# Layer 2's ends: adjacency pieces of the next diffusions loaded further ahead, into the memory of the keys

## The chip, the cores and the metric

The kernel runs on one core of a Trainium2 chip. The metric is the device time of one execution in microseconds (us). A core has TensorE (PE in the profile; its weight loads are PEld), VectorE (DVE), ScalarE (ACT), GpSimd (POOL) and SyncE (SP); SP does no arithmetic here and issues most of the DMAs. Each engine takes its instructions in order.

## The reference

N = 4096 nodes, D = 256 features, an adjacency of zeros and ones. Four layers, each closed by x = layernorm(x + f(x)). Layer 0 is graph attention with 8 heads, layer 1 a product with the adjacency, layer 3 a mean over neighbours with weights. The change lies in layer 2, which is cut here to what matters:

```python
R = S + eye(N); R = R / R.sum(-1, keepdims=True)     # S is the adjacency
Z = 0; Xf = X; Xa = X
for n in range(2):
    A = top_p_attention(Xa, W1, W2, W3)   # softmax of q k^T, only the largest probabilities whose sum
                                          # reaches 0.9 are kept, and renormalised
    Xf = R @ Xf                           # "diffusion"
    Xa = A @ Xa                           # "attention"
    Z = Z + Xf @ U1[n].T + Xa @ U2[n].T
h = X + Z                                 # then a layernorm of h
```

Layer 3 then needs adj @ x for the new x.

## The kernel before, in words

**Tiling.** The 4096 rows are 32 blocks (NB) of 128. In layer 2 the method `layer2` runs two steps, and in each a loop over the blocks b (b = 0 to 30 in the loop, block 31 after it). For a block, 4096 scores lie in one of three buffers `es`; `scores` (L1070) makes those of block b + 2 with matmuls of the queries `q` with the keys `kT`, a tile of 128 x 4096 numbers of 4 bytes (2 MB). `nucleus` (VectorE) finds the cut of a row and clears what lies below; `turn` (L1402, L1404) transposes four 128 x 128 parts of `es` on TensorE and copies them by ScalarE, and `gather` (L1411) multiplies them with X into the PSUM bank `ps_a`. That takes eight sub-steps s = 0 to 7 for a block.

**Pieces.** Beside it runs a diffusion: block b + 2 in step 0, b + 3 in step 1, with `XD` (32 chunks of 128 x 512, the features in two parts) as the moving operand. The adjacency lies in DRAM (`adjs`, with the identity added). A *piece* is four chunks of it, 128 x 512 numbers, 256 KB. `adj_product` (L170 to L180) loads a piece on SP (L177) into the ring `adj_piece` of three buffers, and TensorE multiplies it with four chunks of XD (L180). SP issues its DMAs in order: where a piece has no free buffer, SP waits, and what follows on its queue waits too.

**The ends.** When the last diffusion of a step is through, the first diffusions of what comes next are begun: in step 0 blocks 0 to 2 of step 1, in step 1 blocks 0 to 4 of layer 3. The list `todo` (L1688 on) holds the pairs (block k, piece g) in their order: 21 in step 0, 35 in step 1. `early` (L1619) goes through it. It loads two pieces ahead (`piece`, L1600, into the same ring), and each `next(beside)` in the loop (L1742) issues one more load and multiplies one piece (`times`, L1609). How many pieces fall into which sub-step is written out by hand in `pieces`. In step 1 adjacency pieces on the diagonal need the identity taken off again; GpSimd does that (L1602), and `piece` issues it right after the load. XD is refilled for the new product with `reload` (L1263, on SP), in the order of the table `freed`, which gives for a block and a sub-step the rows to load.

**The flag and the general way.** `settled` (L1291) tests whether the fast way of finding the cuts was right for all rows. Its last parts are two transposes on TensorE (L1314, L1319), a reduction, and a DMA of a row of flags to DRAM (L1323). Then every engine loads the flag (`flag = nc.values_load`, L1809) and branches in `mend` (L1265, L1269): only when the flag is 0 are blocks done again in an exact way, which needs `kT`. In the executions shown the flag isn't 0. `mend` of step 1 also uses `kT` as space for pieces.

**After the branch.** In step 0, `reload` fetches the last four rows of XD, and three pieces (k, 7) finish the diffusions of blocks 0 to 2 (loop over k, L1813 on); then come the last block's attention and the keys of step 1 (`keys`, L941, which writes `kT` anew). In step 1, `early` goes on with pieces 26 to 34 beside the last block's attention; ScalarE unpacks the adjacency of block 5 of layer 3 into `kT` (`cast3`, L1880), and layer 3 (L1956) follows.

**What sets the order.** Inside `tc.manual_schedule` (the loop over b; in step 1 the part after the branch too) the instructions of the five engines stay in the order of the code. Outside it a planner orders them by estimated costs and times; it may also put an instruction from behind the branch ahead of it, if nothing in the branch touches its data. An instruction that depends on what the branch reads or writes stays behind it.

Of the kernel before, what the change touches and what calls it, by code (L numbers as in the profile page):

```python
# [9 lines left out]
F32 = mybir.dt.float32  # L10
# [13 lines left out]
P = 128  # L24
# [31 lines left out]
class Net:  # L56
# [809 lines left out]
    def layer2(self):  # L866
        nc, tc, NB, D, X, N = self.nc, self.tc, self.NB, self.D, self.X, self.N
        A = 64
        HALF = N // 2
        with ExitStack() as ctx:  # L870
# [6 lines left out]
            dram = ctx.enter_context(tc.tile_pool(name="l2d", bufs=1, space=DRAM))  # L877
# [18 lines left out]
            kT = rows2.tile([P, N], F32R, name="kT")  # L896
# [30 lines left out]
            xfd = dram.tile([NB, P, 2, D], F32, name="xfd")  # L927
            xtd = dram.tile([NB, P, 2, D], F32, name="xtd")

            rowd = dram.tile([1, NB + 1], I32, name="rowd")  # L930
            XD = self.XD
            def at(b):
                return bass.ds(b, 1)
# [325 lines left out]
            def reload(src, a, b):  # L1259

                for k in range(a, b, 4):
                    to = min(k + 4, b)
                    nc.sync.dma_start(XD[:, k:to].bitcast(F32), src[k:to].rearrange("b p s d -> p b s d"))  # L1263

            def mend(step, row, flag, e, r, made=()):  # L1265


                spare = es[(NB - 2) % 3][:, :N]
                with tc.If(flag == 0):  # L1269
                    with tc.For_i(0, NB - 1, 1) as b:  # L1270
                        with tc.If(nc.values_load(row[:, at(b)], min_val=0, max_val=1) == 0):
                            e2, Z = exact_scores(b, spare)
                            r2 = exact_nucleus(e2, Z)
                            if step == 1:
                                finish(b, whole(closing(b, attention(e2), r2, bases(b))))
                            else:
                                store(b, attention(e2), r2)
                    with tc.If(nc.values_load(row[:, NB - 1:NB], min_val=0, max_val=1) == 0):
                        e2, Z = exact_scores(NB - 1, e)
                        nc.vector.tensor_copy(r, exact_nucleus(e2, Z))  # L1280
                    if step == 1:
                        reload(xtd, 0, NB - 4)
                        for ps, b, g, first in made:
                            if first:
                                nc.tensor.matmul(ps, kT[:, :P], XD[:, 0].rearrange("p s d -> p (s d)"),
                                                 start=False, stop=True)
                        for i, (ps, b, g, first) in enumerate(made):
                            a = kT[:, i % 8 * 512:i % 8 * 512 + 512].rearrange("p (k i) -> p k i", k=4)
                            times(ps, piece(step, b, g, a), g, first)
# [36 lines left out]
            def exact_scores(b, e):  # L1326

                q = work.tile([P, 2, P], F32R, name="q", bufs=2)
                nc.sync.dma_start(q.bitcast(F32), qd[:, :, bass.ds(b * P, P)])
                for c in range(N // 512):  # L1330
                    pl = bank()
                    for t in range(2):
                        nc.tensor.matmul(pl, q[:, t, :], kT[:, c * 512:(c + 1) * 512], start=(t == 0), stop=(t == 1))
                    nc.scalar.copy(e[:, c * 512:(c + 1) * 512], pl)
                nb = work.tile([P, 1], F32, name="nb", bufs=1)
                nc.vector.tensor_reduce(nb, e, AX.X, ALU.max)
                nc.vector.tensor_scalar(nb, nb, -1.0, LOG_LIFT, op0=ALU.mult, op1=ALU.add)
                Z = work.tile([P, 1], F32, name="Z", bufs=1)
                nc.scalar.activation(e, e, AF.Exp, bias=nb, accum_out=Z)
                return e, Z  # L1340
# [73 lines left out]
            def attention(e):  # L1414


                pa = ps1.tile([P, 512], F32, name="ps_a")
                for g in range(NB // 4):
                    gather(pa, turn(e, g), g)
                return pa  # L1420
# [8 lines left out]
            def base(step, b):  # L1429


                xb = work.tile([P, 2, D], F32, name="xb", bufs=2)
                if step:
                    nc.gpsimd.dma_start(xb[:, 0], xd[b, :, 0, :])
                else:
                    nc.scalar.dma_start(xb[:, 0], pd[b])
                return xb

            def bases(b, queue=nc.scalar):

                xb = work.tile([P, 2, D], F32, name="xb", bufs=2)
                queue.dma_start(xb, xd[at(b)].rearrange("o p s d -> (o p) s d"))
                return xb
# [40 lines left out]
            def whole(steps):  # L1484

                while True:
                    try:
                        next(steps)
                    except StopIteration as end:
                        return end.value  # L1490
# [94 lines left out]
            def finish(b, h, last=False):  # L1585
                whole(ahead3(b, h, weighted(turned(h[:, 0], bank()), bank()), last))
# [8 lines left out]
            def piece(step, b, g, a=None):  # L1595


                if a is None:
                    a = work.tile([P, 4, P], F32R, name="adj_piece", bufs=3)
                nc.sync.dma_start(a.bitcast(F32), self.adjs[b, :, 4 * g:4 * g + 4, :])  # L1600
                if step == 1 and b // 4 == g:
                    nc.gpsimd.tensor_sub(a[:, b % 4, :], a[:, b % 4, :].bitcast(F32), self.ident)  # L1602
                return a

            def times(ps, a, g, first=False, ks=range(4)):

                for k in ks:
                    jc = 4 * g + k
                    nc.tensor.matmul(ps, a[:, k, :], XD[:, jc].rearrange("p s d -> p (s d)"),  # L1609
                                     start=(first and k == 0), stop=(jc == NB - 1))  # L1610
# [7 lines left out]

            def early(step, todo, banks, made):  # L1619

                held = [piece(step, *t) for t in todo[:2]]
                yield
                started = set()
                for i, (b, g) in enumerate(todo):
                    if i + 2 < len(todo):
                        held.append(piece(step, *todo[i + 2]))
                    times(banks[b], held.pop(0), g, b not in started)
                    made.append((banks[b], b, g, b not in started))
                    started.add(b)
                    yield  # L1630

            weights(0)
            for step in range(2):
# [46 lines left out]
                banks, made = {}, []  # L1680
# [7 lines left out]
                if step == 0:  # L1688
                    todo = [(k, g) for g in range(7) for k in range(3)]
                else:  # L1690
                    todo = [(k, g) for g in (1, 2, 3, 4, 5, 0, 6) for k in range(2)]
# [4 lines left out]
                with tc.manual_schedule(engines=five):  # L1696
                    for b in range(NB - 1):
# [14 lines left out]
                        for s in range(8):  # L1712
# [57 lines left out]
                            if s < 6:  # L1770
                                v = result(edge)
                                if v is not None:
                                    rs[b + 1] = v
                            if s == 0 and difs:
                                whole(difs)
                            if s == 4 and not ahead:
# [19 lines left out]
                    b = NB - 1  # L1796
# [13 lines left out]
                mend(step, row, flag, es[b % 3][:, :N], r, made[:] if step else ())  # L1810
                if step == 0:
                    reload(rows_of, NB - 4, NB)
                    sums = [base(1, 0), base(1, 1)]  # L1813
                    for k in range(3):
                        times(banks[k], piece(0, k, 7), 7)
                        if k == 2:
                            sums.append(base(1, 2))
                        whole(diffused(1, k, banks[k], sums[k]))
                        whole(keep(1, k, sums[k]))
                    pa = ps1.tile([P, 512], F32, name="ps_a")  # L1820
                    aTs = [turn(es[b % 3], 0)]
                    found = keys(1, X)
                    next(found)
                    for g in range(8):
                        if g < 7:
                            aTs.append(turn(es[b % 3], g + 1))
                        gather(pa, aTs.pop(0), g)
                        to = min(4 * g + 4, NB - 1)
                        nc.sync.dma_start(X[:, 4 * g:to, :], xad[4 * g:to].rearrange("b p d -> p b d"))
                        if g > 1:  # L1830
                            next(found)
                    nc.scalar.mul(X[:, b, :], pa[:, :D], r)
                    continue

                with tc.manual_schedule(engines=five):
# [8 lines left out]
                    for g in range(8):  # L1844
# [7 lines left out]
                        if g in (2, 4):  # L1852
                            k = NB - 5 + g // 2
# [35 lines left out]
                    for k in range(5):  # L1889
                        t = piece(1, k, 7)  # L1890
# [147 lines left out]
```

## Time and profile before

| what | value |
|---|---|
| median of 3 runs | 3946.61 us (3946.18 to 3950.18) |
| profiled execution, own time | 3947.67 us |
| its span in the profile | 3946.0 us |
| mean granted TensorE clock | 0.994 |
| DMA, whole span | 557.38 MB, mean 141 GB/s |
| end of step 0, 2553.0 to 2607.2: TensorE busy, DMA share | 48.79 of 54.20 us, 0.68 |
| end of step 1, before the branch, 3639 to 3680: TensorE busy | 36.45 of 41 us |
| end of step 1, 3690 to 3746: TensorE busy | 52.43 of 56 us |

The span is what the profiler saw of the program; the execution's own time has a little more around it. A row of waits names the engine, tile and line that stood still, what ended it, the total, how often, and the longest. In a timeline the columns are the start in us from the span's start, the duration, engine, line, operation, tiles, and in brackets the idle time before it with what ended it. "SPq", "POOLq", "PEq" are the sequencers' own instructions: issues of DMAs, branches, register loads.

### The profile page before, as it was taken

How to read it: one execution, taken by the hardware profiler on the slowest of the kernel's cores; microseconds unless marked ns; L12 is line 12 of the kernel's file. 1: busy time of each engine (PE TensorE's matmuls, PEld its weight loads, DVE VectorE, ACT ScalarE, POOL GpSimd, SP SyncE). 2: the span in 40 equal slices, each digit the busy share in tenths (PEclk: the TensorE clock that was granted, in tenths of full speed). 3: DMA queues.
4: the chain of work that ended last, by engine and by line, in shares of the span. 5: the costliest groups of instructions: out<-in, count | busy, mean ns of one | idle time of the engine just before them, and what ended most of it. 6: DMA issues, size and time to landing. Idle time of an engine off the chain costs nothing. (4 is left out here: it accounts for less than half of the span.)

```text
span 3946.0 us, 68781 instructions
## 1 busy us (share of the span) xinstructions
PE 3879.5 (98%) x25081; PEld 3361.6 (85%) x25081; DVE 2993.1 (76%) x6637; ACT 2742.9 (70%) x5121; POOL 1167.5 (30%) x1402
## 2 busy tenths in 40 slices
PE   8999999999999999999999999999999999999898
PEld 7999999999999887578888888866888888888686
DVE  6444449999999444667878788838999999999364
ACT  5434449999998322578888888736888888888232
POOL 1222220111444222311111111114665565555211
PEclk9999999999999999999999999999999999999999
DMA  4666667244221796533332323463333333335541
GB/s 118 204 207 203 219 196 209 82 117 120 77 92 44 281 374 254 148 113 98 98 99 93 103 94 103 156 195 102 102 107 117 105 106 105 117 107 195 199 145 45
DMA packets 317565, 557.38 MB, mean 141 GB/s; under 512 B 72806, under 2 KB 139894, under 8 KB 313110
## 3 DMA queue, kind: packets, MB, share of 16 engines
q1 hardware_dynamic: 242528, 396.99, 30.9%
q0 software_dynamic: 32224, 98.75, 7.7%
q10 hardware_dynamic: 42454, 57.04, 4.2%
q8 instruction: 203, 3.33, 0.3%
q14 instruction: 156, 1.28, 0.1%
HBM read 386.71 MB, written 165.94 MB: 140 GB/s over the span
## 5 line engine op out<-in xcount | busy, mean ns | idle before, releaser
L1411 PE MATMUL ps_a<-X,aT 128*128 128x256 f32 x4096 | 968.9, 379 | 1.3 <-ACT h L1555 1.1
L1411 PEld LDWEIGHTS ps_a<-X,aT 128*128 128x128 f32 x4096 | 773.4, 190 | 127.5 <-issue 3.9
L331 PE MATMUL acc<-gm,gt 128*128 128x198 bf16 x8192 | 701.4, 248 | 11.7 <-DVEq L375 5.3
L331 PEld LDWEIGHTS <-gt 128*128 128x128 fp8e4 x8192 | 699.5, 97 | 13.5 <-issue 7.2
L276 ACT ACTIVATE sg<-lpb,nlc 128x1024 fp8e4<-128x1024 f32 x632 | 663.9, 1135 | 43.4 <-DVE gt L278 29.3
L180 PE MATMUL ps_r<-XD,adj_piece 128*128 128x512 f32 x1888 | 528.4, 414 | 0.0
L601 PE MATMUL pz<-src,ar 128*128 128x264 f32 x4096 | 500.0, 284 | 0.4 <-DVE big L399 0.4
L601 PEld LDWEIGHTS pz<-src,ar 128*128 128x128 f32 x4096 | 499.8, 188 | 0.5 <-issue 0.5
L1138 ACT ACTIVATE ja<-e,nc 128x2048 uint8<-128x2048 f32 x240 | 480.9, 2004 | 2.0
L1404 ACT COPY aT<-ps_tp 128x512 f32<-128x512 f32 x512 | 296.4, 579 | 216.0 <-PE ps_tp L1402 208.7
L180 PEld LDWEIGHTS ps_r<-XD,adj_piece 128*128 128x128 f32 x1888 | 332.9, 189 | 68.8 <-issue 12.9
L1203 DVE MAX8 cand<-v 128x8 f32<-128x256 f32 x1024 | 347.2, 412 | 4.4
L1253 DVE SCALAR_TENSOR_TENSOR e<-e,edge 128x512 f32<-128x512 f32 x512 | 347.6, 750 | 2.1
L561 ACT ACTIVATE nb<-ar 128x512 uint8<-128x512 f32 x256 | 147.6, 623 | 279.5 <-DVE ar L558 170.8
L1402 PE MATMUL ps_tp<-ident,e 128*128 128x128 f32 x2048 | 308.0, 273 | 0.7 <-DVE e L1253 0.7
L1199 DVE SCALAR_TENSOR_TENSOR v<-e,hi 128x2048 f32<-128x2048 f32 x128 | 300.3, 2346 | 2.4
L1402 PEld LDWEIGHTS ps_tp<-ident,e 128*128 128x128 f32 x2048 | 256.8, 142 | 52.1 <-DVE e L1253 0.9
L558 DVE CAST ar<-a 128x1024 fp32r<-128x1024 f32 x128 | 88.9, 694 | 266.7 <-PE pz L601 266.6
L270 DVE TENSOR_SCALAR sg<-lpb,nlc 128x1024 fp8e4<-128x1024 f32 x384 | 285.8, 779 | 6.0 <-SPq L375 3.9
L1047 ACT ACTIVATE e<-ps_logit 128x1024 f32<-128x1024 f32 x256 | 260.2, 1027 | 26.5 <-PE ps_logit L1045 26.3
L1045 PE MATMUL ps_logit<-kT,q 128*128 128x512 f32 x1024 | 274.2, 409 | 1.4 <-ACT e L1047 1.2
L854 PE MATMUL ps_adj<-XD,adj_piece 128*128 128x512 f32 x1024 | 239.8, 394 | 0.0
(404 smaller groups left out, 5599.0 us busy)
## 6 DMA issues: line engine op xcount, KB each, us to landing
adj_piece<-adjs SPq DMA_DIRECT2D x552, 256.0 KB, 2.7
a<-in_adjt_dram SPq DMA_DIRECT2D x256, 256.0 KB, 3.1
adjs<-adj_piece SPq DMA_DIRECT2D x96, 512.0 KB, 3.1
na<-nad SPq DMA_DIRECT2D x64, 512.0 KB, 5.5
lpb<-lpd POOLq DMA_DIRECT2D x32, 512.0 KB, 4.1
nad<-nb POOLq DMA_DIRECT2D x128, 128.0 KB, 2.7
na<-nad ACTq DMA_DIRECT2D x16, 1024.0 KB, 8.8
gmd<-gb POOLq DMA_DIRECT2D x64, 198.0 KB, 2.8
```

What stands on the lines that cost most here:

```text
L180: nc.tensor.matmul(ps, a[:, k, :], rhs(jc).rearrange("p s d -> p (s d)"), start=(jc == 0), stop=(jc == self.NB - 1))
L270: nc.vector.tensor_scalar(sg[:, k, :], lpb, nlc[:, 4 * g + k, h:h + 1], 2.0 ** -5, op0=ALU.is_ge, op1=ALU.mult, saturate=False)
L276: nc.scalar.activation(sg[:, k, :], lpb, AF.Sign, scale=-1.0, bias=nlc[:, 4 * g + k, h:h + 1], saturate=False)
L331: nc.tensor.matmul(acc[:, q, :6 * C1], gt[:, k, q * P:(q + 1) * P], gm0[:, jc, :] if head0 else gm[:, jc, hh, :], start=(jc == 0 and q % 2 ...
L601: nc.tensor.matmul(pz[q][:, t, :W], ar[:, q, k, :], src[:, jc, t, s], start=(jc == 0 and s == 0), stop=(jc == NB - 1 and s == 1))
L1138: nc.scalar.activation(ja, e[:, s * HALF:(s + 1) * HALF], f, bias=nc1, accum_out=fs[:, i + s:i + s + 1])
L1199: nc.vector.scalar_tensor_tensor(v, ec, hi, ec, op0=ALU.is_lt, op1=ALU.mult, accum_out=sb[:, s:s + 1])
L1203: nc.vector.max(cand[:, 8 * j:8 * j + 8], v[:, k * 256:(k + 1) * 256])
L1253: nc.vector.scalar_tensor_tensor(ec, ec, edge[:, j:j + 1], ec, op0=ALU.is_ge, op1=ALU.mult)
L1402: nc.tensor.transpose(pt[:, k * P:(k + 1) * P], e[:, jc * P:(jc + 1) * P], self.ident)
L1404: nc.scalar.copy(aT, pt)
L1411: nc.tensor.matmul(pa[:, :D], aT[:, k * P:(k + 1) * P], X[:, jc, :], start=(jc == 0), stop=(jc == NB - 1))
```

## The change

Four things are changed.

1. In both steps the keys `kT` are copied to DRAM (`kd`) in eight parts of 256 KB, one in each of the blocks b = 2 to 9 at s = 5, on SP. In `mend`, when the flag is 0, SP loads them back first.
2. `early` loads up to six pieces ahead of the one that it multiplies, into eight slots of 512 columns in `kT` (`key_slot`), free from the last scores on. In step 0 that holds for all 21 pieces. In step 1 pieces 0 and 1 go to the ring as before, pieces 2 to 25 go to the slots, and pieces 26 to 34 to the ring, two ahead, as before.
3. With a load, the identity's subtraction in step 1 (in `piece`) moves to the earlier place as well.
4. In step 0 the three pieces (k, 7) after the branch are loaded together ahead of the loop over k, into slots 5 to 7 of `kT`.

```diff
+            kd = dram.tile([N // 512, P, 512], F32, name="kd")
...
                 with tc.If(flag == 0):
+                    for i in range(N // 512):
+                        nc.sync.dma_start(kT[:, i * 512:(i + 1) * 512].bitcast(F32), kd[i])
...
+            def key_slot(i):
+
+                i = i % 8 * 512
+                return kT[:, i:i + 512].rearrange("p (k i) -> p k i", k=4)
...
             def early(step, todo, banks, made):
 
-                held = [piece(step, *t) for t in todo[:2]]
-                yield
+                held, issued, until = [], 0, 26 if step else len(todo)
                 started = set()
-                for i, (b, g) in enumerate(todo):
-                    if i + 2 < len(todo):
-                        held.append(piece(step, *todo[i + 2]))
+                for i in range(-1, len(todo)):
+                    while issued < len(todo) and issued <= i + (6 if 2 * step <= issued < until and i + 1 >= step else 2):
+                        in_keys = 2 * step <= issued < until
+                        held.append(piece(step, *todo[issued], key_slot(issued) if in_keys else None))
+                        issued += 1
+                    if i < 0:
+                        yield
+                        continue
+                    b, g = todo[i]
                     times(banks[b], held.pop(0), g, b not in started)
                     made.append((banks[b], b, g, b not in started))
                     started.add(b)
...
+                            if s == 5 and 2 <= b < 2 + N // 512:
+                                cols = slice((b - 2) * 512, (b - 1) * 512)
+                                nc.sync.dma_start(kd[b - 2], kT[:, cols].bitcast(F32))
...
                     reload(rows_of, NB - 4, NB)
+                    ends = [piece(0, k, 7, key_slot(5 + k)) for k in range(3)]
                     sums = [base(1, 0), base(1, 1)]
                     for k in range(3):
-                        times(banks[k], piece(0, k, 7), 7)
+                        times(banks[k], ends[k], 7)
```

## The prediction

> **What bounds the kernel now.** I read the page first: busy time of each engine.
>
> ```profile
> PE 3879.5 (98%) x25081; PEld 3361.6 (85%) x25081; DVE 2993.1 (76%) x6637; ACT 2742.9 (70%) x5121; POOL 1167.5 (30%) x1402
> ```
>
> TensorE is busy for 98% of the span, so a change that removes no matmul can only gain where TensorE stands still. Next I asked the waits of TensorE around the two places that the diff touches: the end of step 0 (2500 to 2720 us) and of step 1 (3580 to 3750 us). Columns: total us, times, longest.
>
> ```profile
> PE ps_logit L1609 <- DMA adj_piece<-adjs: 4.8, 5, 2.6
> ...
> PE ps_r L1609 <- PEq L1269: 0.3, 1, 0.3
> ```
>
> ```profile
> PE ps_logit L1609 <- DMA adj_piece<-adjs: 5.8, 5, 1.7
> PE ps_tp L1495 <- PEq L1269: 4.2, 1, 4.2
> PE ps_logit L1609 <- POOLq L1269: 1.9, 1, 1.9
> ```
>
> Line 1609 multiplies the early pieces, 1269 is the branch of `mend` on the flag. So the two ends hold 10.6 us of waiting for pieces, and some 6 us around the branch. Between them, in 2690 to 3590 us, TensorE's waits come to 0.7 us. Third, the timeline, to see why a piece is late. Step 0 (start, duration, engine, line):
>
> ```profile
> 2583.65 0.42 SPq L1263 DMA_DIRECT2D XD<-xfd  x1
> ...
> 2586.05 11.57 SPq L1600 DMA_DIRECT2D adj_piece<-adjs  x6
> ...
> 2588.61 0.18 PE L1319 MATMUL ps_tp<-ident,each 32*1 32x32 f32 x1
> ...
> 2592.49 2.14 PE L1609 MATMUL ps_logit<-XD,adj_piece 128*128 128x512 f32 x8 [2.57 <-DMA adj_piece<-adjs]
> ...
> 2594.93 1.18 PE L1609 MATMUL ps_r<-XD,adj_piece 128*128 128x512 f32 x4 [0.30 <-PEq L1269]
> ```
>
> The piece issued at 2586.05 sits in SP's queue behind a reload of 1 MB, could not be issued before a ring buffer was free, and is used at 2592.49, 6.4 us after its issue. The flag's loads in step 0 show who was ready for the branch:
>
> ```profile
> L1809 ACTq TENSOR_LOAD <-rowd x1: 1115/1115/1115, 2590.7 to 2590.7; - x1
> ...
> L1809 PEldq TENSOR_LOAD <-rowd x1: 665/665/665, 2593.1 to 2593.1; - x1
> L1809 SPq TENSOR_LOAD <-rowd x1: 766/766/766, 2594.1 to 2594.1; - x1
> ```
>
> The flag was in DRAM by 2590.7; TensorE and SP came later, because both stood at pieces. Step 1:
>
> ```profile
> 3673.88 0.45 POOL L1602 TENSOR_TENSOR adj_piece<-adj_piece,ident 128x128 fp32r<-128x128 f32 x1
> 3674.38 2.64 PEld L1609 LDWEIGHTS ps_logit<-XD,adj_piece 128*128 128x128 f32 x12 [2.38 <-POOLq L1269]
> ...
> 3678.55 1.20 PE L1609 MATMUL ps_logit<-XD,adj_piece 128*128 128x512 f32 x4 [1.09 <-DMA adj_piece<-adjs]
> ```
>
> The wait named POOLq is not the branch: it is GpSimd's subtraction of the identity (L1602) from piece (4,1), which stands behind the closing's 2.06 us add of 3671.86.
>
> [...]after the 4.2 us wait the stage 3680 to 3690 has a granted clock of 0.66. [...]the branch takes 0.36 us in step 0 and 3.77 us in step 1. [...]
>
> **The change, part by part.** The waits' column understates, since a matmul's modelled end overlaps the next start; I use start to start. Four undelayed matmuls of a piece take 1.02 us (2569.77 to 2570.79).
>
> *Step 0, loop.* Pieces start 2.18 us apart at 2566.65 (from 2564.47) and 1.98 at 2578.01 (from 2576.03): 1.16 + 0.96 = 2.1 us over. With eight slots and six loads issued ahead a piece leaves when the eighth before it is used, about 14 us ahead (piece 0 starts at 2555.25, piece 8 at 2570.79), against 5 to 9 us of landing in this crowded stretch (98% DMA share at 2543 to 2555). Both go. VectorE's `okay`, which L1314 needs, ends at 2575.85, long before 2584.81: nothing else is late.
>
> *Step 0, to the branch.* From L1319 (2588.61) to the first matmul after the branch (2594.93) are 6.32 us. TensorE's own work there is three pieces, 3.1 us; the flag is at hand 2.1 us after L1319 (2590.7), and from TensorE's load of it to its matmul are 1.83 us (2593.1 to 2594.93): 3.9 us. The later ends it: 3.9. Saved 2.4; 0.8 of the stall turns into waiting for the flag.
>
> *Step 0, `ends`.* Their three loads write kT, which the general branch reads and writes, so they cannot leave SP before it. Today the first leaves at 2593.72, before SP's branch, and is used at 2596.80. SP needs 2.0 us from its load of the flag to a DMA (2594.1 to 2596.07) and, no longer stuck, loads the flag 2.1 us after L1319: issue at 4.1, landing at 4.1 + 3.1 = 7.2. TensorE wants the piece at 3.9 + 1.0 (last piece) + 0.4 (a turn) = 5.3: 1.9 us of stall in today's order, none if the planner puts a turn and a gather (2.1 us) first. I take 1.0, against 0.7 today (0.26 + 0.19 + 0.27): a loss of 0.3, ends +0.7 and -1.2.
>
> *Step 1, before the branch.* Start to start: 2.43 at 3643.40 (1.4 over), 3.04 at 3674.38 (2.0 over), 4.17 instead of 3.06 at 3678.55 (1.1 over): 4.5 us. Pieces 2 to 25 leave six ahead, and the subtraction moves with them: that of (4,1) is queued on GpSimd at s = 5, before the closing's add. Behind the subtractions GpSimd holds `above` (3659.19), needed by VectorE at 3663.02; the slot of piece (3,0) is free at about 3654.3 and the slowest landing of a piece here is 6.2 us, so it comes by 3660.5 and nobody waits. `okay` ends at 3665.49; L1314, today 3667.31, comes 1.4 earlier: 0.4 us of slack left. Piece 2 waits for the last reading of kT, about 3614.1, and is used at 3624.18. All 4.5 go.
>
> *Step 1, branch and after.* TensorE reaches its branch late even so[...]: gain 0. Pieces 26 to 34 keep the ring of three, so the waits at 3714.99, 3717.14 and 3726.38 stay: 0.
>
> *Sixteen copies of keys to DRAM.* No such copy is in the trace. Nearest rows: xtd<-part, also 256 KB, lands in 2.7 us; an SP issue costs 0.32. A gain is excluded, as it only adds traffic. In the loops a piece leaves 5.92 us before its first matmul at the least and lands in 2.7: 3.2 us of cover, against 0.4 of issue and, at the 390 GB/s seen near 2543, 0.7 of transfer. I take 0; without cover the copies cost up to 16 x 1.1 = 18 us. The general branch's reload isn't executed[...].
>
> *Sum.* 2.1 + 2.4 - 0.3 + 4.5 = 8.7 us. The profiled execution took 3947.67 (span 3946.0 and 1.7 around it), 1.06 over the median; it becomes 3939.0, the median 3946.61 - 8.7 = 3937.9. The half-clock stretches (6.8 us at 2658.9 and at 3682.9, 3.4 at 3717.1 and 3727.3) [...]a stretch of 3.4 us more or less is worth up to 1.7. The planner also reorders what lies outside the hand-ordered parts; I give both together +-2.
>
> **Rivals.**
> - *The branch takes over.* [...]only the stalls ahead of L1319 count, 2.1 + 1.4, less 1.2 at `ends`, is 2.3; with half of step 1's later 3.1 it is 3.8: 3942.8. For it: ACT stood ready at the branch at once. Against: TensorE's load at 3678.6 came 6.8 us after the flag's at 3671.8.
> - *More goes than counted.* The planner covers `ends` (+1.3), [...]and 3.4 us of half clock fall away (1.7): 3.5 more: 3934.4. For it: SP's queue is empty earlier[...].
> - *The copies delay the loop.* A copy stands ahead of pieces in SP's queue. It decides above 8.7 / 16 = 0.54 us for each copy, that is if the piece behind it lands 3.7 us late; at 1.1 us it is 17.6 - 8.7 = +8.9: 3955.5. Against: the cover of 3.2 us and a DMA that moves only some 100 GB/s there.
> - *It doesn't do it:* pieces leave no sooner because SP is held by reloads ahead of them. The reloads' own waits end by 2583.65, and the pieces to 17 stand before that; this ends between 3942 and 3946, and I count it with the first rival.
>
> **How the numbers follow.** Forecast 0.55, first rival 0.25, second 0.15, third 0.05. 0.2% is 7.9 us, about what a measurement here can tell from no change: the bound is 3938.7. Of the forecast's 0.55 about 0.40 lie under it, with 0.15 of the second rival: faster 0.55, same 0.40, slower 0.05. The range goes from inside the second rival to past the first, 3933.5 to 3943.5.
>
> **What would show it.** Right: in step 0 no wait for DMA at 1609 before the flag, the branch following L1319 by 3.9 us; in step 1 no POOLq wait and no DMA wait before the branch, with 4.2 us at it still; L180 without waits in both loops. Wrong: DMA waits at L180 in the first third of a loop (copies), L1314 later than its predecessor's end (`okay`), or a wait of over 2 us at `ends`.

## The result, and the profile after

| | before | after |
|---|---|---|
| median of 7 runs each | 3946.61 us (3944.54 to 3950.18) | 3932.46 us (3929.16 to 3934.97) |
| profiled execution, its span | 3947.67, 3946.0 us | 3932.46, 3930.8 us |
| ratio after to before, 95% interval | | 0.9962 [0.9953, 0.9971] |

The medians lie 14.2 us apart; the ratio over all runs makes it 15.0 us (11.4 to 18.5). Predicted were 8.7. The direction was right, the size was not: 3932.46 lies below the range of 3933.5 to 3943.5.

The page's line of busy times, after:

```profile
PE 3872.5 (99%) x25081; PEld 3360.1 (85%) x25081; DVE 2995.1 (76%) x6637; ACT 2742.3 (70%) x5121; POOL 1162.8 (30%) x1402
```

The counts are those of before. TensorE is busy for 7.0 us less although it does the same matmuls; so a part of the 15.2 us that the span lost is not waiting, but matmuls that take less time. The prediction's opening, that a change without fewer matmuls can gain only where TensorE stands still, had left that out. The waits of TensorE after, first in 2500 to 2720 us, then in 3580 to 3740 us:

```profile
PE ps_tp L1405 <- DVEq L1270: 1.7, 1, 1.7
...
```

```profile
PE ps_logit L1617 <- DMA adj_piece<-adjs: 3.3, 4, 1.3
PE ps_tp L1498 <- PEq L1270: 0.8, 1, 0.8
```

(Lines 1609, 1269, 1319, 1402 and 1495 of before are now 1617, 1270, 1322, 1405 and 1498.) In step 0 no piece is waited for. In step 1 the pieces cost 3.3 us, all after the branch. The surprise is the last row: TensorE stands at the branch for 0.8 us instead of 4.2, which the prediction had left as it was.

**Where the time went.** The trace is the same program up to small shifts, so I followed single matmuls through both profiles and took start after minus start before. A growing minus is time gained.

| stretch of the profile | gained in it, us | predicted |
|---|---|---|
| step 0, to L1322 | 3.2 | 2.1 |
| step 0, L1322 to the first turn of step 1's loop | 1.9 | 2.4 - 0.3 |
| step 1, to L1322 | 1.6 | 1.4 |
| step 1, L1322 to the first matmul after the branch | 7.2 | 2.0 + 1.1 |
| step 1, the 21 us after the branch | 2.4 | 0 |
| step 1, from there to layer 3 | 2.8 | 0 |

The table sums to 19.1, the spans' difference is 15.2: where it begins, at 2540 us, the profile after is 3.9 us behind. 3.0 of them are there by 758 us, in layer 0, which the change doesn't touch: two stretches of half clock (granted clock 0.5, at 575 and 589 us) last 6.8 us each instead of 3.4 in this one profile. One profile against one carries such chance; the experiments below settle the shares.

**Step 1's branch**, last transpose (L1322) to the first matmul after the branch, timeline after:

```profile
3667.37 0.18 PE L1322 MATMUL ps_tp<-ident,each 32*1 32x32 f32 x1
...
3668.51 4.70 PE L1617 MATMUL ps_logit<-XD,kT 128*128 128x512 f32 x20
3673.97 0.41 PE L1498 MATMUL ps_tp<-ident,h 128*128 128x128 f32 x2 [0.76 <-PEq L1270]
```

It took 6.60 us (3667.37 to 3673.97); before it was 13.80 (3670.18 to 3683.98), with the same 24 matmuls in between. By TensorE's *sequencer* I mean what the profile lists as its own instructions (PEq, PEldq: the load of the flag, the branch), by the *array* what does the matmuls. The loads of the flag show when each sequencer came that far. Columns: line, engine, operation, count, shortest/median/longest in ns, first and last start. Before, then after:

```profile
L1809 ACTq TENSOR_LOAD <-rowd x1: 634/634/634, 3671.8 to 3671.8; - x1
...
L1809 PEldq TENSOR_LOAD <-rowd x1: 1022/1022/1022, 3678.6 to 3678.6; - x1
```

```profile
L1825 ACTq TENSOR_LOAD <-rowd x1: 637/637/637, 3669.0 to 3669.0; - x1
...
L1825 PEldq TENSOR_LOAD <-rowd x1: 516/516/516, 3669.0 to 3669.0; - x1
```

And the branch itself, before and after:

```profile
L1269 PEldq COMPARE_BRANCH  x1: 3768/3768/3768, 3679.7 to 3679.7; - x1
```

```profile
L1270 PEldq COMPARE_BRANCH  x1: 3888/3888/3888, 3669.6 to 3669.6; - x1
```

The branch is no shorter. The traces show its 3.8 us and not what fills them. But after, TensorE's sequencer loads the flag at 3669.0, while the array still has matmuls to do until 3673.2: they were handed over already. The branch runs beside them. Before, the sequencer stood at the weight load (PEld) of the late piece, which was let go at 3678.55:

```profile
3678.55 0.76 PEld L1609 LDWEIGHTS ps_logit<-XD,adj_piece 128*128 128x128 f32 x4 [1.53 <-DMA adj_piece<-adjs]
```

It loaded the flag at 3678.6 and took the branch while the array had only that one piece left. The late piece cost its own wait, and the cover of the branch as well.

**The clock after the branch.** Stretch, length, busy time and count of PE, PEld, DVE, ACT, POOL, granted clock, DMA share, GB/s; before, then after:

```profile
3680.00:3690.00 10.00, 6.02 (x16) 3.67 (x17) 0.00 (x0) 1.54 (x3) 0.72 (x1) 0.66 0.65 233
```

```profile
3673.00:3680.00 7.00, 6.17 (x30) 4.30 (x30) 0.61 (x2) 1.81 (x4) 3.48 (x5) 1.00 0.79 300
```

After a wait of 0.76 us no clock is lost; with one of 4.23, from 3682.9 on, it was at half for 6.8 us.

**Step 0's branch**, timeline after:

```profile
2589.33 0.18 PE L1322 MATMUL ps_tp<-ident,each 32*1 32x32 f32 x1
...
2592.30 1.07 PE L1617 MATMUL ps_r<-XD,kT 128*128 128x512 f32 x4
2595.03 1.06 PE L1405 MATMUL ps_tp<-ident,e 128*128 128x128 f32 x8 [1.67 <-DVEq L1270]
```

All of the loop's pieces are handed over before the branch now; the planner put the last one, which TensorE took behind the branch before (2594.93), ahead of it. The first matmul behind it is a turn, 5.70 us after L1322 (2589.33 to 2595.03), where it was 7.33 (2588.61 to 2595.94). It waits for VectorE, whose sequencer branches at 2591.7 and goes on at 2594.9:

```profile
L1270 DVEq EVENT_SEMAPHORE  x2: 21/21/21, 2594.9 to 2595.0; - x2
...
L1270 DVEq COMPARE_BRANCH  x1: 63/63/63, 2591.7 to 2591.7; - x1
```

This was so before, too (2591.9 and 2595.4, 3.5 us).

### The profile page after: what moved, and what is told of

The parts are those of the page before. It is cut to its first block, busy times and chain, and to the rows that moved or that the text cites. A ratio compares the mean times of both kernels' runs of the same rounds, so it can differ in the third digit from the quotient of the medians.

```text
span 3930.8 us, 68793 instructions
## 1 busy us (share of the span) xinstructions
PE 3872.5 (99%) x25081; PEld 3360.1 (85%) x25081; DVE 2995.1 (76%) x6637; ACT 2742.3 (70%) x5121; POOL 1162.8 (30%) x1402
## 3 DMA queue, kind: packets, MB, share of 16 engines
q14 instruction: 157, 1.28, 0.1%
## 5 line engine op out<-in xcount | busy, mean ns | idle before, releaser
L180 PE MATMUL ps_r<-XD,adj_piece 128*128 128x512 f32 x1888 | 528.4, 414 | 0.0
L180 PEld LDWEIGHTS ps_r<-XD,adj_piece 128*128 128x128 f32 x1888 | 333.0, 189 | 68.8 <-issue 12.9
```

Of the source, the lines that this page charges most:

```text
L180: nc.tensor.matmul(ps, a[:, k, :], rhs(jc).rearrange("p s d -> p (s d)"), start=(jc == 0), stop=(jc == self.NB - 1))
```

## The experiments

Two theories. **The sequencer theory**: the piece that is late last before a branch holds TensorE's sequencer; on time, the branch's 3.8 us run beside matmuls that were handed over, and the half clock after the wait goes too. **The piece theory** is the rival: the branch's shorter wait and the faster tail are the luck of this profile, and the change is worth its waits for pieces alone. The kernels ran on three chips; medians of before there: 3946.24 (of 35 runs; rows 1 to 4), 3946.74 (rows 5 to 8) and 3947.41 (rows 9 to 12). The last column is the difference of the medians on the same chip, with the interval from the ratio of all runs.

| kernel | median us (lowest to highest) | against before, us [95%] |
|---|---|---|
| step 0 alone | 3940.17 (3937.94 to 3945.33) | -6.1 [-8.3, -3.2] |
| step 1 alone | 3934.61 (3932.42 to 3938.98) | -11.6 [-17.0, -8.3] |
| copies alone | 3947.88 (3945.18 to 3951.03) | +1.6 [-1.6, +5.1] |
| piece 25 in the place of 22 | 3933.06 (3928.75 to 3934.30) | -13.2 [-20.5, -9.9] |
| piece 25 late | 3937.31 (3934.43 to 3942.93) | -9.4 [-13.8, -6.3] |
| two ahead, eight slots | 3933.23 (3931.88 to 3934.59) | -13.5 [-20.1, -9.1] |
| before, no branch in step 1 | 3942.56 (3937.63 to 3947.75) | -4.2 [-6.3, -1.2] |
| after, no branch in step 1 | 3930.51 (3926.26 to 3933.49) | -16.2 [-22.9, -12.2] |
| the `ends` as before | 3932.18 (3928.52 to 3934.06) | -15.2 [-20.5, -9.5] |
| four pieces of step 1 | 3940.12 (3934.54 to 3945.23) | -7.3 [-11.1, -3.6] |
| the tail too | 3927.17 (3922.40 to 3928.06) | -20.2 [-25.7, -15.0] |
| the changed kernel again | 3933.16 (3931.30 to 3936.54) | -14.3 [-18.9, -8.3] |

**The parts alone.** Step 0 alone (the copies and the reload only there too):

```diff
-                held, issued, until = [], 0, 26 if step else len(todo)
+                held, issued, until = [], 0, 0 if step else len(todo)
```

> The change in step 0 alone (keys copied, pieces and the three last ones in the keys' memory in step 0; step 1 as before). Sequencer theory: TensorE's sequencer runs ahead of the array as soon as no piece holds it, [...]and the half clock that followed the idle goes too; most of the gain lies in step 1. Then this kernel gains about 5 us (3941 to 3942), and step 1 has its 4.2 us at the branch and a half-clock stretch after it as before. Piece theory (the prediction's: only the waits for pieces count[...]): 4 to 5 us here too, but then it is about half of the whole gain.

Step 1 alone (the copies and the reload only there), `ends` as before:

```diff
-                held, issued, until = [], 0, 26 if step else len(todo)
+                held, issued, until = [], 0, 26 if step else 0
...
-                        times(banks[k], ends[k], 7)
+                        times(banks[k], piece(0, k, 7), 7)
```

> The change in step 1 alone (step 0 as before). Sequencer theory: 9 to 14 us (3933 to 3937): 4.5 of pieces, 3.5 at the branch, 2 to 2.5 of half clock right after it and up to 2.8 in the tail; the wait at the branch is below 1 us. Piece theory: 4.5 us (3942), the branch still waits about 4 us.

Copies alone: `until = 0`, `ends` as before, copies and reload kept.

> The copies of the keys to DRAM and their reload in the general branch alone; no piece lies in the keys' memory. Both theories: within 1.5 us of before, no wait of L180 for a piece in the loops. The rival of the prediction (copies delay the loop): up to 18 us slower.

Step 0 gives 6.1 us and step 1 gives 11.6; their sum of 17.7 agrees with 14.2 inside the intervals. Predicted were 4.2 and 4.5, so the missing gain lies mainly in step 1. The copies cost nothing that can be measured. The waits with step 0 alone, 3580 to 3745 us, show the waits for the branch and for GpSimd much as before (4.2 and 1.9 there), and less waiting for pieces (3.0 against 5.8):

```profile
PE ps_tp L1498 <- PEq L1270: 3.8, 1, 3.8
PE ps_logit L1617 <- DMA adj_piece<-adjs: 3.0, 4, 1.5
PE ps_logit L1617 <- POOLq L1270: 1.9, 1, 1.9
```

With step 1 alone the row of the branch is this:

```profile
PE ps_tp L1498 <- PEq L1270: 1.1, 1, 1.1
```

The short wait comes with step 1's slots, not with luck. Step 0 alone shows something more. The array, at half clock from 3672.1 to 3675.5 (granted clock 0.77 in 3670 to 3680), takes the last 16 matmuls before the branch there without a gap:

```profile
3670.67 5.54 PE L1617 MATMUL ps_logit<-XD,adj_piece 128*128 128x512 f32 x16 [1.95 <-POOLq L1270]
```

```profile
L1825 PEldq TENSOR_LOAD <-rowd x1: 501/501/501, 3674.6 to 3674.6; - x1
```

No matmul waits for the last piece. Only its weight load stands for 0.30 us, until 3674.57; the flag is loaded then, though ScalarE loads it at 3668.1, and the branch's wait is 3.8 us. A piece can thus be on time for the array and too late for the sequencer.

**One late piece.** If one late piece is enough to hold the sequencer, then delaying piece 25 alone must bring the long wait back. The first attempt:

```diff
-                        held.append(piece(step, *todo[issued], key_slot(issued) if in_keys else None))
+                        held.append(piece(step, *todo[issued], key_slot(22 if step and issued == 25 else issued) if in_keys else None))
```

> The change, but piece 25 of step 1, the last one ahead of the branch, gets the slot of piece 22, so that its load can only leave when piece 22 is used. Sequencer theory: piece 25 comes 1 to 2 us late, TensorE's sequencer stands at it[...]: the wait at the branch comes back with 3 to 4 us, 4 to 6 us slower than the changed kernel, more if the half clock comes back. Piece theory: slower by the late piece alone, 1 to 2 us, the wait at the branch stays below 1 us.

This was a miss of mine. In the code the load of piece 25 stands before the multiplication of piece 22, so it overwrote piece 22's data early instead of waiting for its reader (piece 22 is multiplied with piece 25's adjacency: that part of the computation is changed), and nothing came late. The wait at the branch is 0.8 us and the time that of the changed kernel. It says nothing on the theory. Second attempt, with the load issued two ahead, behind that multiplication:

```diff
-                held, issued, until = [], 0, 26 if step else len(todo)
+                held, issued, until = [], 0, 25 if step else len(todo)
...
+                        held.append(piece(step, *todo[issued], key_slot(issued) if in_keys else key_slot(22) if step and issued == 25 else None))
```

> The change, but piece 25 of step 1, the last one ahead of the branch, is loaded two ahead and into the slot of piece 22, so that its load can only leave when piece 22 has been multiplied. Sequencer theory: it comes 1.5 to 2 us late, TensorE's sequencer stands at it[...]: the wait at the branch comes back with 3 to 4 us, and a half-clock stretch with it; 5 to 7 us slower than the changed kernel (3937 to 3940). Piece theory: slower by the late piece alone, 1.5 to 2 us (3934 to 3935), the wait at the branch stays below 1 us.

Timeline and TensorE's load of the flag in that kernel:

```profile
3666.99 0.18 PE L1322 MATMUL ps_tp<-ident,each 32*1 32x32 f32 x1
...
3672.81 1.20 PE L1617 MATMUL ps_logit<-XD,kT 128*128 128x512 f32 x4 [0.88 <-DMA kT<-adjs]
3677.39 0.41 PE L1498 MATMUL ps_tp<-ident,h 128*128 128x128 f32 x2 [3.39 <-PEq L1270]
```

```profile
L1825 ACTq TENSOR_LOAD <-rowd x1: 634/634/634, 3668.6 to 3668.6; - x1
...
L1825 PEldq TENSOR_LOAD <-rowd x1: 622/622/622, 3672.8 to 3672.8; - x1
```

Piece 25 is only 0.88 us late. TensorE loads the flag at 3672.8, the moment at which that piece arrives, though ScalarE loads it at 3668.6; the branch's wait is 3.39 us again, followed by 3.4 us at half clock (granted clock 0.76 in 3677 to 3684). From L1322 to the matmul after the branch it takes 10.40 us instead of 6.60: 0.88 of lateness costs 3.8 us there. Its runs (3934.43 to 3942.93) lie 4.1 us in the median above the kernel with two ahead on the same chip (3931.88 to 3934.59), whose piece 25 is on time at the branch; the changed kernel itself did not run on that chip. 5 to 7 us over the changed kernel were expected.

**Only the last four pieces** (22 to 25) of step 1 in slots, step 0 as before:

```diff
-                    while issued < len(todo) and issued <= i + (6 if 2 * step <= issued < until and i + 1 >= step else 2):
-                        in_keys = 2 * step <= issued < until
+                    while issued < len(todo) and issued <= i + (6 if 22 * step <= issued < until and i + 1 >= step else 2):
+                        in_keys = 22 * step <= issued < until
```

> Step 1 alone, and only pieces 22 to 25, the last four ahead of the branch, in the keys' memory; pieces 0 to 21 go to the ring two ahead, step 0 is as before. Sequencer theory: what counts is that nothing holds TensorE's sequencer just ahead of the branch. [...]8 to 11 us, 3936 to 3939, the wait at the branch below 1.2 us. Piece theory: 3.1 us (3943.5).

The 8 to 11 us were the waits of 2.0 and 1.1 us, 3.5 us less of waiting at the branch and the half clock after it.

```profile
3670.83 0.18 PE L1322 MATMUL ps_tp<-ident,each 32*1 32x32 f32 x1
...
3678.82 0.55 PE L1498 MATMUL ps_tp<-ident,h 128*128 128x128 f32 x2 [2.10 <-PEq L1270]
```

7.99 us from L1322 to after the branch: four pieces bring 5.8 of the 7.2. But the wait at the branch is 2.1 us and the gain 7.3, where less than 1.2 and 8 to 11 were expected. The rest is the flag, which reached all engines 3.1 us after L1322 here (3673.9) and 1.6 us after it in the changed kernel. Its DMA left at the same distance from L1322 in both (0.5 us), but took 2.5 us instead of 1.1 from there to the loads. The DMA engines' busy share in that time was 0.81 (3671.4 to 3673.9), with pieces under way, and 0.00 in the changed kernel (3667.9 to 3669.0). So crowded DMA engines are the likely reason; no run tests it.

**Order or slots.** Two ahead in the code as before, but still in eight slots:

```diff
-                    while issued < len(todo) and issued <= i + (6 if 2 * step <= issued < until and i + 1 >= step else 2):
+                    while issued < len(todo) and issued <= i + (2 if 2 * step <= issued < until and i + 1 >= step else 2):
```

> The change with pieces issued two ahead in the code's order, as before, instead of six, but still into the eight slots. SP isn't bound to the array's place, only to free slots, so both theories expect the loads to leave nearly as early: no DMA wait ahead of the branch in step 1. The subtraction of piece (4,1) is back behind the closing's add: a wait named POOLq of 1 to 2 us. Sequencer theory: some 2 us slower than the changed kernel (3934 to 3936)[...]. Piece theory: 2 us as well; if six ahead in the code is what matters, 6 us or more slower.

```profile
PE ps_logit L1617 <- DMA adj_piece<-adjs: 3.7, 3, 1.8
PE ps_logit L1617 <- POOLq L1270: 2.0, 1, 2.0
PE ps_tp L1498 <- PEq L1270: 0.9, 1, 0.9
```

The time is that of the changed kernel (3933.23 against 3932.46 and 3933.16 on other chips), where 3934 to 3936 were expected. SP was held back by full buffers, not by the place of the load in the code. The wait for GpSimd is back, since its subtraction stands behind the closing's add again. But it ends at 3668.72 with 16 matmuls to come, none of which waits for anything; they are handed over, and the branch's wait stays at 0.9 us. From L1322 to after the branch it takes 9.07 us (3664.52 to 3673.59) against 6.60: the order has 2.5 us in this place of the profile, which the runs can't tell.

**What the branch is worth.** The same edit in before and in after; step 1's flag, its branch and the general way of step 1 are left out:

```diff
-                flag = nc.values_load(row[:, NB:], min_val=0, max_val=1)
-                mend(step, row, flag, es[b % 3][:, :N], r, made[:] if step else ())
+                if step == 0:
+                    flag = nc.values_load(row[:, NB:], min_val=0, max_val=1)
+                    mend(step, row, flag, es[b % 3][:, :N], r, made[:] if step else ())
```

> The kernel before without the loading of the flag, the branch and the general way of step 1 (left out; the flags are still computed and written). Both theories: the 4.2 us at the branch go, and with the idle the half clock after it, 2 us: 3939 to 3941; the waits for pieces stay.

> The changed kernel without the loading of the flag, the branch and the general way of step 1 (left out). Sequencer theory: the branch is hidden in the changed kernel already, so leaving it out gives at most 1 us (3931 to 3933). Piece theory, by which the branch's 4.2 us are still paid and the gain lies elsewhere: 4 to 6 us (3927 to 3929).

Without the branch, before gains 4.2 us (1.2 to 6.3), less than the 6 to 7 expected. After stands 2.7 us under the kernel with two ahead on the same chip, with runs that overlap; that is more than the 1 us of the sequencer theory and less than the 4 to 6 of the piece theory. So this pair of runs doesn't decide. It isn't a pure test either: without the branch, transposes from behind it (L1495, L1402) stand among the last pieces of before, and its wait for GpSimd falls to 1.0 us. What decides between the theories is the late piece and the parts alone.

**The `ends`** in the ring, one load ahead of each product as before, the rest changed:

```diff
-                    ends = [piece(0, k, 7, key_slot(5 + k)) for k in range(3)]
...
-                        times(banks[k], ends[k], 7)
+                        times(banks[k], piece(0, k, 7), 7)
```

> The change, but the three pieces (k, 7) after step 0's branch are loaded as before, each in its turn and into the ring, so that they may be put ahead of the branch. The prediction's term: 0.3 us faster than the changed kernel, at most 1.5. Both theories: within 1.5 us of the changed kernel (3931 to 3934).

3932.18 against 3933.16 of the changed kernel on the same chip: no difference that can be seen.

**The tail too.** Behind step 1's branch pieces 28 to 31 go to a free buffer `v`, and pieces are loaded up to six ahead; four of the five pieces (k, 7) go to `v` as well:

```diff
-                    while issued < len(todo) and issued <= i + (6 if 2 * step <= issued < until and i + 1 >= step else 2):
+                    while issued < len(todo) and issued <= i + (6 if (2 * step <= issued < until or step and i > 25) and i + 1 >= step else 2):
...
+                        if step and issued == 28:
+                            tail.append(work.tile([P, 4, 4, P], F32R, name="v", bufs=1))
+                        slot = key_slot(issued) if in_keys else tail[0][:, issued - 28] if step and 28 <= issued < 32 else None
+                        held.append(piece(step, *todo[issued], slot))
...
-                        t = piece(1, k, 7)
+                        t = piece(1, k, 7, tail[0][:, k] if k < 4 else None)
```

> The change, and behind step 1's branch pieces 28 to 31 and four of the five pieces (k, 7) go into the memory of VectorE's scratch tile v, which is dead by then, up to six ahead. The four waits for pieces in the tail, 3.3 to 3.7 us together, go: 3 to 4 us faster than the changed kernel (3928 to 3930), and no half-clock stretch in the tail. If the closing chain of the last block ends last there, less than 1 us.

> The changed kernel once more, beside the other three on the same chip, as their measure: 3931 to 3935, 13 to 15 us below the kernel before.

The tail of the changed kernel still waits for pieces (in brackets), as predicted; here with the same stretch of the kernel with the tail changed below it:

```profile
3702.56 1.21 PE L1617 MATMUL ps_logit<-XD,adj_piece 128*128 128x512 f32 x4 [0.81 <-DMA adj_piece<-adjs]
3704.39 2.48 PE L1617 MATMUL ps_logit<-XD,adj_piece 128*128 128x512 f32 x8 [0.62 <-DMA adj_piece<-adjs]
...
3712.16 0.97 PE L1617 MATMUL ps_logit<-XD,adj_piece 128*128 128x512 f32 x3 [1.28 <-DMA adj_piece<-adjs]
```

```profile
3699.46 2.97 PE L1617 MATMUL ps_logit<-XD,adj_piece 128*128 128x512 f32 x12
```

No piece is waited for any more, and this kernel is the fastest: 6.0 us under the changed kernel on the same chip, with runs that don't overlap (the highest 3928.06, the lowest of the changed kernel 3931.30). The waits it removes are 3.3 us, and 3 to 4 were expected; I take the rest for clock that the tail's waits cost in some executions, but no run separates it.

**All profiles together.** One profile's clock is partly chance, so I took the two stretches over all of them. From step 0's last undelayed piece to the first turn of step 1's loop, the nine kernels with step 0's loads early gain 6.4 us on the profile of before in the mean, and the five with step 0 as before (its own, at 0, among them) 0.8: step 0 is worth 5.6. From the loop of step 1 to layer 3, the six with the changed step 1 and its branch gain 12.5, and the three with step 1 as before 3.2 (the profile of before had 6.8 us of half clock in the tail that the other two lacked): step 1 is worth 9.3. Together 14.9, against 14.2 to 15.0 from the runs. The scatter is wide: without the profile of before, whose tail was slow, step 1 would be worth 7.7.

## Why the prediction was right or wrong

**The step that failed**: "*Step 1, branch and after.* TensorE reaches its branch late even so", with the gain of 0 that it puts there: the branch's 3.77 us were to be paid in full, as before. That is wrong. The branch is no shorter, 3.89 us, but TensorE's sequencer reaches it early, and the array stands still for only 0.76 us of it; with the piece's own wait gone, this place gained 7.2 us instead of 3.1. I had read the branch from the array's side, where it follows the last piece; it had to be read from the sequencer's. The flag's loads, which I showed for step 0 and not for step 1, told it: 3678.6 is not the end of the last piece but the moment at which its weight load was let go. In step 0 I even used that reading. What follows for the sum: the last transpose to after the branch takes what the flag takes (1.6 us), the load of it (0.6), and the branch and the first matmul (about 4.4), 6.60 in all, against 5.8 of matmuls. With that, 7.2 instead of 3.1 could have been written down.

**The clock**, which the prediction gave to chance ("a stretch of 3.4 us more or less"), partly follows from the same cause. In all five profiles with a wait over 2 us at step 1's branch (4.2, 3.8, 3.7, 3.4, 2.1) 3.4 or 6.8 us at half clock begin in the wait or up to 0.3 us after it; in the seven with at most 1.2 us none does, nor around that place in the two without the branch. The length of a wait doesn't settle it alone: the wait for GpSimd of 1.95 us was followed by 3.4 us at half clock 1.4 us later in step 0 alone, and by none at that place in three other profiles with the same wait; and in the tail waits of 1.2 to 1.5 us came just ahead of half clock in four profiles, but not in the changed kernel's (1.28). The shortest wait at the branch that half clock followed is the 2.1 us with four pieces in slots; what sets where a stretch begins, the runs don't show. In the profile of before two matmuls of L1609 start 0.427 us apart at half clock (3717.7 to 3720.3) instead of about 0.235 at full (3722.4 to 3724.3), so 6.8 us of such matmuls lose about 3. The clock in the tail, 2.8 of the table, is chance for the larger part: it comes and goes between kernels with the same tail (6.8 us at half clock in the profile of before, none in the other two with step 1 as before).

**The rest by its steps.**
- *Step 0's loop*, 2.1 predicted, 3.2 found. The waits went. The rest was not counted: with pieces in time the second and third piece in a row start 0.92 us after the one before, instead of the 1.02 I took for undelayed ones.
- *Step 0 to the branch*, 2.4 less 0.3 predicted, 1.9 found. The first matmul after the branch doesn't follow L1322 by the predicted 3.9 us: it is 5.70, and the end is set by VectorE, which goes on 3.2 us after its branch, not by TensorE. The sum had no term for VectorE, though the profile before has it at 3.5 us. The planner took a piece from behind the branch ahead of it, so less was left behind, and that the total came out near is luck in part.
- *`ends`*, 0.3 of loss predicted: no wait for DMA there, the planner put two turns and their products first, as one case of the prediction had it.
- *Before the branch in step 1*, 4.5 predicted: the waits all went. The slack of 0.4 us at `okay` was too little to count on: in the changed kernel's first profile L1317 doesn't wait, but in five others it waits 0.4 to 1.2 us for it.
- *The tail's waits stay*: right, 3.3 us in four.
- *Sixteen copies at 0*: right. A copy lands in 3.4 us, where 2.7 were taken from a similar transfer, and L180 has no waits in the loops; in both stretches with copies every turn of the changed kernel keeps its distance from the same turn of before (3.88 us later in step 0, 1.18 earlier in step 1). The rival of the slower side, +8.9, did not come.

```profile
L1789 SPq DMA_DIRECT2D kd<-kT x16: 383/426/935, 1771.2 to 3013.2; - x16
...
DMA to landing us min/median/max: 3.3/3.4/3.4
```

The second rival ("more goes than counted", 3934.4) was right that half clock falls away: it took 3.4 us, and the 6.8 behind step 1's branch are gone. It gave TensorE's branch at most 1 us, and for a shorter one, which it isn't: 3.77 us before and 3.89 after.

**Open**: what fills the 3.8 us of TensorE's branch, whether crowded DMA engines delayed the flag with four pieces in slots, how much of step 1's gain and of the tail's is clock, and what VectorE does in the 3.2 us after its branch.

## What to carry to other kernels

A wait just ahead of a branch can cost more than its own length: here 0.88 us cost 3.8, since it held the sequencer, and the branch then found almost no handed-over work to hide beside. Look up when the sequencer reaches the branch, not when the array ends, and keep the last few microseconds of work ahead of it free of waits. Where loads come late, count the buffers before moving the loads in the code; here eight buffers with the old order gave all of the gain that the runs can tell.

## What the hardware showed that was not expected

- TensorE's sequencer took a branch of 3.89 us while the array did the matmuls handed over before it (3668.51 to 3673.2); the array stood still for only 0.76 us.
- A piece that was 0.88 us late cost 3.8 us to the matmul after the branch. One that no matmul waited for, whose weight load stood for 0.30 us, still brought a wait of 3.8 us at the branch.
- After step 0's branch VectorE went on only 3.2 us later (2591.7 to 2594.9; before, 2591.9 to 2595.4), while TensorE's branch there took 0.36 us in both kernels.
- A wait of 2.1 us at step 1's branch was followed by half clock, waits of 1.2 us and less at the same place were not; elsewhere waits of 1.2 to 2.0 us were in some executions and not in others.
